# Softmax denominators folded through DRAM instead of on TensorE, and a recurrence started from halves

## The chip, the cores and the metric

The kernel runs on one core of one Trainium2 chip. Its engines have names here: PE (TensorE, the matrix engine; PEld is its weight loads), DVE (VectorE), ACT (ScalarE), POOL (GpSimd) and SP (SyncE, which here only issues DMA transfers). SBUF is the on-chip memory of 128 partitions, PSUM the accumulator that PE writes, DRAM the memory off the core. Everything is float32. The metric is the device time of one execution in microseconds, the median of several.

## What is computed

The input x has 4 batches of 128 channels and 64 x 64 = 4096 positions. Three stages follow one another.

```
# layer 0, per batch, xf = x[b] as (128 channels, 4096 positions)
q, k, v = wq @ xf, wk @ xf, wv @ xf              # 64 rows each
att = softmax(k.T @ q, axis=keys)                # 4096 x 4096
x = x + wo @ (att @ v.T).T
# layer 1, per batch, t = x as (4096 tokens, 128)
h = layernorm(t)
t = t + softmax(causal(h Wq (h Wk).T / sqrt(128))) @ (h Wv)
# last stage, a recurrence over the 4096 tokens of each batch
wx = batchnorm(layernorm(t) @ W.T)               # statistics over all batches and tokens
y[n] = sigmoid(wx[n] + y[n-1] @ V.T),  y[-1] = 0
out = t + y
```

Of each softmax the kernel divides only at the end: it forms the sum of exp(score) x value over the keys, the sum of exp(score) over the keys (the denominator of a query), and multiplies the first by the reciprocal of the second.

## The kernel before

The main program is fast_path. A second one, general_path, is in the program as well and runs only when a flag is set at the end, if a denominator leaves its range or the recurrence has not converged.

**Work items.** For each batch there are 8 blocks of 512 queries in layer 0 and then 8 in layer 1. A block is cut into items of two tiles of 128 keys: 16 items in each block of layer 0, and 2, 4, ... 16 in the causal blocks of layer 1. An item is handled in three steps: scores (L753: PE makes s_ps, ACT takes exp into p), sums (L794: DVE adds p into dsum, L804, or copies it for a block's first item, L802) and values (L814: PE adds p times the values into acc). One slot of the loop at L896 holds scores of item s, values of item s-2 and sums of item s. There are four buffers for p and two of PSUM for s_ps, one for acc, and two ("misc") that all other PE products share.

**The end of a block.** When the last item has its values (L839), ACT copies acc (half at L843 in layer 0, agg at L846 in layer 1), DVE adds the halves (agg, L844) and brings the two halves of dsum together in den (L848): 128 partitions by 512 queries, where a partition holds the sum over the keys that lie on it. What is missing is the sum over the 128 partitions, with the result on the partition of its query. DVE transposes den in squares of 32 x 32 (folded, L556) and adds 32 neighbours (part, L558): part has, on partition 32k + r, for each of the 4 x 4 groups of 32 queries, the sum over the k-th quarter of the keys. In project the matrix fold adds the four quarters on PE (den_ps, L567), and as every partition then holds the sums of its row of all four groups, DVE multiplies by a mask (quarter, L569) and adds (L570) to keep its own group's. The reciprocal follows (recs, L571), the output product o_ps on PE (L574), and the scaled addition into xs (L579). Then comes the layer norm (normed, L588 to L595; POOL takes the power at L455), a transposition into squares (sqT, L609) and an exchange through DRAM that makes the transposed tokens xhT: by_r in layer 0 (L642, L647: four writes, four reads), by_c in layer 1 (L702, L706: four writes, one read). In layer 1 the last step is third (L708): wx_ps on PE, its statistics on DVE (L713), and ACT's copy into xs (L722).

**The order.** These steps are chains of generators: `yield n, step` means that the step comes n slots later; one step runs at the end of a slot, the earliest due first, and if none is due, a task of the side list (the next batch's keys and values). In layer 0 the folding comes one slot after the block's end, the rest (project and what follows) at the end of the next block. In layer 1 the chain is

```
yield 1, first       # folded, project, store to x2, normed
yield 3, second      # squares, exchange
yield 1 if final else 4, third
```

with final the last block of the last batch. From the program so written the framework makes one list of instructions for each engine, with a scheduler of its own that may move an instruction up or down its engine's list where the data allow. Every engine works its list in order, and an instruction that has to wait holds up those behind it. All transfers of the main loop are issued by SP.

**The recurrence** (L972 to L995) is cut into 256 chunks of 16 tokens for each batch, all taken side by side. A chunk's starting state comes from WARM = 12 warm-up steps over the tokens ahead of it. The first has no previous state and is only a sigmoid (L982); every other step is a product on PE (L985), an addition on DVE (L987) and a sigmoid on ACT (L990) for each of the four batches. With the 16 steps proper that makes 28 rounds. At the end the state that a chunk reaches is compared with the one that the next chunk was started from (L1014 to L1025); in_range (L612) counts the reciprocals that lie between two bounds into good. Both set the flag.

Of the kernel before, what the change touches and what calls it, by code (L numbers as in the profile page):

```python
# [349 lines left out]
def fast_path(  # L350
# [27 lines left out]
    TPB = BLK // P  # L378
    SHIFT = 32.0
    LOW, HIGH = 1e-25, 1e25  # L380
    WARM, TOL, STEPS = 12, 1e-6, 16
    NCH = N // STEPS
    CPB = BLK // STEPS
    S = nc.vector.STREAM_SQUARE_SIZE
# [45 lines left out]
    for q in range(1, Q):  # L430
        nc.vector.tensor_copy(fold[:, ts(q, S)], fold[:, :S])

    quarter = const.tile([P, TPB, Q], F32, name="quarter")
    for j in range(TPB):
        nc.vector.tensor_reduce(quarter[:, j], ident.rearrange("p (q r) -> p q r", r=S), AX.X, ALU.add)
# [8 lines left out]
    good = const.tile([P, 1], F32, name="good")  # L444
# [5 lines left out]
    nc.gpsimd.memset(ends[:, 0:1], float((B * NB - 1) * BLK))  # L450
    spare = const.tile([P, 1], F32, name="spare")

    def rsqrt(y, var, z):
# [7 lines left out]
    with tc.tile_pool(name="batch", bufs=1) as batch, tc.tile_pool(name="rows", bufs=2) as rowp, tc.tile_pool(  # L461
# [7 lines left out]
        def misc(name):  # L469
            return ps_m.tile([P, BLK], F32, tag="m", name=name)  # L470
# [2 lines left out]
        wp = misc("warm_ps")  # L473
        for _ in range(12):
            nc.tensor.matmul(wp[:, :P], lhsT=ident, rhs=ident, start=True, stop=True)

        def form():
            gp = misc("g_ps")
# [71 lines left out]
            nc.scalar.copy(r, ps)  # L550
            bs[b].next.append(r)

        def folded(den):

            sq = wk.tile([P, TPB * Q, S], F32, tag="sq", name="sq")
            nc.vector.transpose(out=sq.rearrange("p a b -> p (a b)"), in_=den)  # L556
            part = stat.tile([P, TPB * Q], F32, tag="part", name="part")
            nc.vector.tensor_reduce(part, sq, AX.X, ALU.add)  # L558
            return part

        def project(layer, b, g, agg, part):

            dp = misc("den_ps")
            rec = recs[:, layer, b, ts(g, TPB)]


            nc.tensor.matmul(dp[:, : TPB * Q], lhsT=fold, rhs=part, start=True, stop=True)  # L567
            own = stat.tile([P, TPB, Q], F32, tag="own", name="own")
            nc.vector.tensor_tensor(own, dp[:, : TPB * Q].rearrange("p (j q) -> p j q", q=Q), quarter, ALU.mult)  # L569
            nc.vector.tensor_reduce(rec, own, AX.X, ALU.add)  # L570
            nc.vector.reciprocal(rec, rec)  # L571
            op = misc("o_ps")
            for j in range(TPB):
                nc.tensor.matmul(  # L574
                    op[:, ts(j, P)], lhsT=agg[:, ts(j, P)], rhs=wv1 if layer else wo2, start=True, stop=True
                )
# [35 lines left out]
        def in_range():  # L612

            r = recs.rearrange("p l b t -> p (l b t)")
            r2 = wk.tile([P, BLK], F32, tag="den", name="r2")[:, : 2 * B * NT]
# [3 lines left out]
            nc.vector.tensor_reduce(good, r, AX.X, ALU.add)  # L619

        def ahead():

# [5 lines left out]
        def finish0(b, g):  # L628

            agg, den = bs[b].agg, bs[b].den  # L630

            def norm():
                if g == 0:
                    bs[b].xh = batch.tile([P, NT, P], F32, tag="xh", name="xh")
                    bs[b].xhT = batch.tile([P, N], F32, tag="xhT", name="xhT")
                normed(b, g, bs[b].xh[:, ts(g, TPB)])

            def by_channels():
                sq = squares(bs[b].xh[:, ts(g, TPB)])
                by_r = dram2.tile([S, Q, TPB, Q, S], F32, tag="by_r", name="by_r")  # L640
                for q in range(Q):
                    nc.sync.dma_start(  # L642
                        out=by_r[:, :, :, q].rearrange("r c j t -> r (c j) t"),
                        in_=sq[ts(q, S)].rearrange("r c j t -> r (c j) t"),
                    )
                for c in range(Q):
                    nc.sync.dma_start(  # L647
                        out=bs[b].xhT[ts(c, S), ts(g, BLK)], in_=by_r[:, c].rearrange("r j q t -> r (j q t)")
                    )

            def rest():
                yield 1, norm
                yield 2, by_channels

            def first():
                part = folded(den)

                def second(s):
                    project(0, b, g, agg, part)
                    push(s, rest())  # L660

                fill.append(second)

            yield 1, first

        def finish1(b, g):
# [10 lines left out]
            def first():  # L677
                if final:

                    nc.scalar.activation(spare, agg[:, 0:1], AF.Sigmoid)  # L680
                project(1, b, g, agg, folded(den))
                if final:
                    warm(9, agg[:, : BLK // 2])
                nc.sync.dma_start(
                    out=x2[b, ts(g, BLK)].rearrange("(j p) c -> p j c", p=P),
                    in_=xs[:, b, ts(g, BLK)].rearrange("p (j c) -> p j c", c=P),
                )
                mem["xh"] = wk.tile([P, TPB, P], F32, tag="xh2", name="xh2")
                normed(b, g, mem["xh"])
# [18 lines left out]
            def third():  # L708
                wp = misc("wx_ps")
                nc.tensor.matmul(wp, lhsT=wf, rhs=mem["xhT"], start=True, stop=True)  # L710
                if b == B - 1 and g == NB - 1:
                    in_range()
                nc.vector.bn_stats(ends[:, 3:] if final else stats[:, b * NB + g], wp)  # L713
                if b == B - 1 and g == NB - 2:
                    ahead()

                to = xs[:, b, ts(g, BLK)]
                if final:
                    nc.scalar.copy(to.rearrange("p (s c) -> p s c", c=CPB), wp.rearrange("p (c s) -> p s c", s=STEPS))
                    warm(6, to[:, : BLK // 2])  # L720
                else:
                    nc.scalar.copy(  # L722
                        to.rearrange("p (s j q u) -> p s j q u", q=Q, j=TPB, s=STEPS),
                        wp.rearrange("p (q j u s) -> p s j q u", q=Q, j=TPB, s=STEPS),
                    )

            yield 1, first
            yield 3, second
            yield 1 if final else 4, third


        class Item:
# [163 lines left out]
        for s in range(len(items) + SKEW + 16):  # L896
# [20 lines left out]
            if due:  # L917
                w = min(due, key=lambda w: w[0])
                waiting.remove(w)
                w[1]()  # L920
                push(s, w[2])
            elif side:
                side.pop(0)()
                if not side and items[s].b == 0 and items[s].layer == 0:
                    tokens()
                    load_rest()
        assert not waiting and not side and not fill


# [4 lines left out]
    with tc.tile_pool(name="xr", bufs=1) as xrp, tc.tile_pool(name="y", bufs=2) as yp, tc.tile_pool(  # L934
# [17 lines left out]
        shift = xrp.tile([P, 1], F32, name="shift")  # L952
        nc.vector.tensor_tensor(shift, mv[:, 0:1], scale, ALU.mult)
        nc.vector.tensor_tensor(shift, beta, shift, ALU.subtract)

        by_step = xs.rearrange("p b (g s c) -> p b s g c", s=STEPS, c=CPB)
        start = xrp.tile([P, B, NCH + 1], F32, name="start")
# [14 lines left out]
        def step(b, s):  # L972
# [6 lines left out]
            else:  # L979
                y = states(b, s)  # L980
            if prev[b] is None:
                nc.scalar.activation(grid(y), wx, AF.Sigmoid, scale=scale, bias=shift)  # L982
            else:
                ps = ps_y.tile([P, NCH], F32, tag=f"y{b}", name="y_ps")
                nc.tensor.matmul(ps if s < 1 else pair(ps), lhsT=vf, rhs=prev[b], start=True, stop=True)  # L985
                z = yp.tile([P, NCH], F32, tag=f"z{b}", name="z")
                nc.vector.scalar_tensor_tensor(  # L987
                    grid(z), in0=wx, scalar=scale, in1=grid(ps), op0=ALU.mult, op1=ALU.add
                )
                nc.scalar.activation(y, z if s < 0 else pair(z), AF.Sigmoid, bias=shift)  # L990
# [24 lines left out]
        for b in range(B):  # L1015
# [5 lines left out]
        count = xrp.tile([P, B + 1], F32, name="count")  # L1021
# [68 lines left out]
```

## Time and profile before

| | |
|---|---|
| median of three runs | 2115.99 us (2115.71 to 2116.8) |
| the profiled execution | 2116.78 us, its span in the trace 2115.1 us |
| PE busy | 2081.9 us (98%) |
| DVE busy | 1501.6 us (71%) |
| ACT busy | 1009.5 us (48%) |
| POOL busy | 112.2 us (5%) |
| fold product on PE (L567), 64 times | 128 matmul passes, mean 240 ns |
| product with the mask on DVE (L569) | 64 times, mean 164 ns |
| reduction (L570), reciprocal (L571) | 64 times each, mean 166 and 177 ns |
| dsum additions of 128 x 1024 (L804) | 676 times, mean 1221 ns |
| recurrence step on DVE (L987) | 108 times, mean 480 ns |

The span is the time from the first to the last record; the few microseconds around it belong to the execution too. A line of the profile with an arrow, such as "[0.66 <-ACT p L778]", means that the engine stood idle for 0.66 us and that the event which ended this was ACT writing p. A matmul of float32 is two passes, so counts on PE are twice the program's, and since matmuls are pipelined a pass's own duration overlaps the next; what a product costs PE is seen from one start to the next.

### The profile page before, as it was taken

The numbers are of one execution on the slowest core, as the hardware profiler recorded it, in microseconds if no ns is written. First come the engines' busy times: TensorE is split into PE (matmuls) and PEld (weight loads), VectorE is DVE, ScalarE is ACT, GpSimd is POOL, SyncE is SP. The second block draws the span as 40 slices with busy tenths as digits, with TensorE's granted clock in tenths as the row PEclk, the third lists the DMA queues.
The fourth block names the chain that finished last, engine by engine and source line by source line (L and its number), as shares of the span: only waits on it lengthen the run. The fifth ranks groups of instructions, "written<-read, shape, count | busy, mean of one in ns | idle before, by whom it ended". The sixth has DMA issues, their size and how long they took to land. (4 is left out here: it accounts for less than half of the span.)

```text
span 2115.1 us, 30710 instructions
## 1 busy us (share of the span) xinstructions
PE 2081.9 (98%) x11880; PEld 918.3 (43%) x11880; DVE 1501.6 (71%) x2906; ACT 1009.5 (48%) x1099; POOL 112.2 (5%) x220
## 2 busy tenths in 40 slices
PE   9999999999999999999999999999999999999998
PEld 3333354444333344444333335444433334544456
DVE  4898875555788986545689988554478998754578
ACT  5666633333666643333466653333356664333355
POOL 1000010000000001000000001000000000100000
PEclk9999999999999999999999999999999999999999
DMA  3100022000100012100010002210000001110043
GB/s 111 51 21 12 21 70 60 26 15 15 56 21 15 18 36 70 51 24 15 16 51 15 18 21 62 63 30 15 15 16 15 17 21 26 50 31 15 15 164 161
DMA packets 139897, 81.79 MB, mean 39 GB/s; under 512 B 75248, under 2 KB 123888, under 8 KB 138720
## 3 DMA queue, kind: packets, MB, share of 16 engines
q1 hardware_dynamic: 138736, 79.20, 13.1%
q8 instruction: 95, 1.56, 0.3%
q14 instruction: 58, 0.48, 0.1%
q0 software_dynamic: 288, 0.39, 0.1%
q10 hardware_dynamic: 720, 0.16, 0.0%
HBM read 42.24 MB, written 33.29 MB: 36 GB/s over the span
## 5 line engine op out<-in xcount | busy, mean ns | idle before, releaser
L804 DVE TENSOR_TENSOR dsum<-dsum,p 128x1024 f32<-128x1024 f32 x676 | 825.1, 1221 | 409.9 <-ACT p L780 305.7
L778 ACT ACTIVATE p<-s_ps,nshift 128x1024 f32<-128x1024 f32 x512 | 571.3, 1116 | 350.4 <-PE s_ps L764 292.4
L764 PE MATMUL s_ps<-kr 64*64 64x512 f32 x2048 | 570.4, 594 | 5.0 <-ACT p L778 5.0
L824 PE MATMUL acc<-p,v 64*64 64x512 f32 x4096 | 572.9, 592 | 1.7 <-ACT half L843 1.7
L780 ACT ACTIVATE p<-s_ps 128x1024 f32<-128x1024 f32 (+2 forms) x288 | 274.6, 953 | 555.3 <-PE s_ps L773 526.3
L764 PE MATMUL s_ps<-swap,kr 64*64 64x512 f32 x2048 | 530.2, 594 | 1.0 <-DMA swap<-kr 0.9
L773 PE MATMUL s_ps<-rows,xhT 128*128 128x512 f32 (+3 forms) x1152 | 503.7, 559 | 0.0
L832 PE MATMUL acc<-p,xh 128*128 128x512 f32 (+3 forms) x1152 | 501.9, 558 | 0.2
L832 PEld LDWEIGHTS acc<-p,xh 128*128 128x128 f32 x1152 | 215.8, 190 | 243.1 <-issue 230.4
L773 PEld LDWEIGHTS s_ps<-rows,xhT 128*128 128x128 f32 x1152 | 213.2, 190 | 240.2 <-issue 202.9
L824 PEld LDWEIGHTS acc<-p,v 64*64 64x64 f32 x4096 | 169.4, 133 | 281.9 <-issue 274.0
L764 PEld LDWEIGHTS s_ps<-kr 64*64 64x64 f32 x2048 | 152.3, 133 | 143.6 <-issue 122.4
L764 PEld LDWEIGHTS s_ps<-swap,kr 64*64 64x64 f32 x2048 | 138.6, 133 | 139.3 <-issue 125.3
L455 POOL TENSOR_TENSOR ln_rstd<-ln_var,mhalf 128x4 f32<-128x4 f32 x64 | 66.2, 1035 | 1076.4 <-DVE ln_var L591 1076.4
L812 DVE TENSOR_TENSOR dsum<-dsum,p 128x256 f32<-128x256 f32 (+1 forms) x120 | 55.9, 501 | 75.5 <-POOL p L784 75.5
L579 DVE SCALAR_TENSOR_TENSOR xs<-o_ps,recs,xs 128x128 f32<-128x128 f32 x256 | 71.9, 343 | 7.4 <-PE o_ps L574 3.7
L595 DVE TENSOR_SCALAR xh<-xs,ln_mv,ln_rstd 128x128 f32<-128x128 f32 x256 | 71.4, 342 | 2.3
L784 POOL TENSOR_SCALAR_AFFINE_SELECT p<-p 128x128 f32<-128x128 f32 x128 | 35.2, 299 | 652.2 <-ACT p L780 642.5
L588 DVE BATCH_NORM_STATS2 ln_st<-xs 128x6 f32<-128x128 f32 x256 | 63.4, 269 | 0.0
L722 ACT COPY xs<-wx_ps 128x512 f32<-128x512 f32 x31 | 18.2, 586 | 80.6 <-DVE stats L713 80.6
L802 DVE COPY dsum<-p 128x1024 f32<-128x1024 f32 x60 | 41.1, 686 | 20.2 <-ACT p L780 15.9
L987 DVE SCALAR_TENSOR_TENSOR z<-xs,scale,y_ps 128x256 f32<-128x256 f32 x108 | 48.3, 480 | 3.3 <-PE y_ps L985 1.9
(132 smaller groups left out, 1054.7 us busy)
## 6 DMA issues: line engine op xcount, KB each, us to landing
xs<-in_xT SPq DMA_DIRECT2D x32, 256.0 KB, 3.0
by_r<-sqT SPq DMA_DIRECT2D x128, 64.0 KB, 2.2
xhT<-by_r SPq DMA_DIRECT2D x128, 64.0 KB, 2.0
x<-xs SPq DMA_DIRECT2D x32, 256.0 KB, 2.2
xr<-x SPq DMA_DIRECT2D x8, 1024.0 KB, 12.5
out_x<-xr SPq DMA_DIRECT2D x16, 512.0 KB, 4.4
by_c<-sqT SPq DMA_DIRECT2D x124, 64.0 KB, 1.8
xhT<-by_c SPq DMA_DIRECT2D x31, 256.0 KB, 2.6
```

What stands on the lines that cost most here:

```text
L455: nc.gpsimd.tensor_tensor(y, var, mhalf[:, : y.shape[-1]], ALU.pow)
L579: nc.vector.scalar_tensor_tensor(t, in0=op[:, ts(j, P)], scalar=rec[:, j : j + 1], in1=t, op0=ALU.mult, op1=ALU.add)
L588: nc.vector.bn_stats(st[:, j], xs[:, b, ds(g * BLK + j * P, P)])
L595: nc.vector.tensor_scalar(dst[:, j], xs[:, b, ds(g * BLK + j * P, P)], mv[:, j, 0:1], y[:, j : j + 1], ALU.subtract, ALU.mult)
L764: nc.tensor.matmul(ps[c * M : c * M + M, off : off + n], lhsT=bs[it.b].kr[part, h, ds(t % (NT // 2) * P + c * M, M)], rhs=rows[h], start=True,
L773: nc.tensor.matmul(ps[:, off : off + n], lhsT=lhsT, rhs=rhs, start=True, stop=True)
L778: nc.scalar.activation(it.p[:, :off], ps[:, :off], AF.Exp, bias=nshift)
L780: nc.scalar.activation(it.p[:, :off], ps[:, :off], AF.Exp, scale=float(P) ** -0.5)
L804: nc.vector.tensor_tensor(flat, flat, it.p, ALU.add)
L812: nc.vector.tensor_tensor(den[:, h, q0:], den[:, h, q0:], it.p[:, o : o + n], ALU.add)
L824: nc.tensor.matmul(bt.acc[h * M : h * M + M, r], lhsT=bt.v[part, t], rhs=it.p[part, o : o + n], start=it.first, stop=it.last,)
L832: nc.tensor.matmul(bt.acc[:, 0, q0:], lhsT=bt.xh[:, t], rhs=it.p[:, o : o + n], start=it.first and h == 0, stop=it.last and h == 1,)
```

## The change

Four things are changed in fast_path.

1. In layer 0's blocks, and in layer 1's from the third on (all but the last of the last batch), the four quarters in part are no longer added on PE. part is written to a DRAM tile by_token in four transfers, one from each quarter of the partitions, so that it lies there by token, and read back in one as own: 128 partitions, each with the four quarters of its own four queries. In all that is 32 + 24 - 1 = 55 blocks, each with four writes of 2 KB in pieces of 16 bytes, and one read of 8 KB. The multiplication by the mask is not needed there; the addition of the four (now over quarters) and the reciprocal remain. The nine other blocks keep the product and the mask, with the two dimensions in another order.
2. In layer 1 the chain is given new distances: folding one slot after the block's end, then, where the quarters go through DRAM, first two slots after that; third of the first two blocks comes 6 slots after second instead of 4.
3. The recurrence starts from a state of 0.5 everywhere: V's product with a column of halves is formed once near the start (form_half), added to the bias of the first sigmoid (shift_half), and WARM is 11.
4. The test of the reciprocals' range is done in two parts: all but the last block's four columns after the last block but one, these four at the end.

```diff
-    WARM, TOL, STEPS = 12, 1e-6, 16
+    WARM, TOL, STEPS = 11, 1e-6, 16
...
+        def form_half():
+            hp = misc("h_ps")
+            nc.tensor.matmul(hp[:, 0:1], lhsT=vf, rhs=point5, start=True, stop=True)
+            nc.vector.tensor_copy(v_half, hp[:, 0:1])
...
-        def folded(den):
+        def folded(den, by_pe):
...
-            nc.vector.tensor_reduce(part, sq, AX.X, ALU.add)
-            return part
+            nc.vector.tensor_reduce(part, sq.rearrange("p j q s -> p q j s"), AX.X, ALU.add)
+            own = stat.tile([P, Q, TPB], F32, tag="own", name="own")
+            if by_pe:
+                dp = misc("den_ps")[:, : TPB * Q]
+                nc.tensor.matmul(dp, lhsT=fold, rhs=part.rearrange("p q j -> p (q j)"), start=True, stop=True)
+                nc.vector.tensor_tensor(own, dp.rearrange("p (q j) -> p q j", q=Q), quarter, ALU.mult)
+            else:
+                by_token = dram2.tile([Q, S, Q, TPB], F32, tag="by_token", name="by_token")
+                for k in range(Q):
+                    nc.sync.dma_start(out=by_token[:, :, k].rearrange("q r j -> r q j"), in_=part[ts(k, S)])
+                nc.sync.dma_start(out=own, in_=by_token.rearrange("q r k j -> (q r) k j"))
+            return own
...
-        def project(layer, b, g, agg, part):
-            dp = misc("den_ps")
+        def project(layer, b, g, agg, own):
             rec = recs[:, layer, b, ts(g, TPB)]
-            nc.tensor.matmul(dp[:, : TPB * Q], lhsT=fold, rhs=part, start=True, stop=True)
-            own = stat.tile([P, TPB, Q], F32, tag="own", name="own")
-            nc.vector.tensor_tensor(own, dp[:, : TPB * Q].rearrange("p (j q) -> p j q", q=Q), quarter, ALU.mult)
-            nc.vector.tensor_reduce(rec, own, AX.X, ALU.add)
+            nc.vector.tensor_reduce(rec, own.rearrange("p q j -> p j q"), AX.X, ALU.add)
             nc.vector.reciprocal(rec, rec)
...
             def first():
-                part = folded(den)
+                own = folded(den, False)
                 def second(s):
-                    project(0, b, g, agg, part)
+                    project(0, b, g, agg, own)
...
-                project(1, b, g, agg, folded(den))
+                project(1, b, g, agg, mem["own"])
...
                 if b == B - 1 and g == NB - 1:
-                    in_range()
+                    in_range(True)
...
                 if b == B - 1 and g == NB - 2:
                     ahead()
+                    in_range(False)
...
-            yield 1, first
+            by_pe = final or g < 2
+            def sums():
+                mem["own"] = folded(den, by_pe)
+            if by_pe:
+                yield 1, lambda: (sums(), first())
+            else:
+                yield 1, sums
+                yield 2, first
             yield 3, second
-            yield 1 if final else 4, third
+            yield 1 if final else 6 if g < 2 else 4, third
...
+        shift_half = xrp.tile([P, 1], F32, name="shift_half")
+        nc.vector.tensor_tensor(shift_half, shift, v_half, ALU.add)
...
-                nc.scalar.activation(grid(y), wx, AF.Sigmoid, scale=scale, bias=shift)
+                nc.scalar.activation(grid(y), wx, AF.Sigmoid, scale=scale, bias=shift_half)
```

More of the change, by code (lines that the diff above doesn't have):

```diff
@@ L431, in fast_path @@
         nc.vector.tensor_copy(fold[:, ts(q, S)], fold[:, :S])
-    quarter = const.tile([P, TPB, Q], F32, name="quarter")
+    quarter = const.tile([P, Q, TPB], F32, name="quarter")
     for j in range(TPB):
-        nc.vector.tensor_reduce(quarter[:, j], ident.rearrange("p (q r) -> p q r", r=S), AX.X, ALU.add)
+        nc.vector.tensor_reduce(quarter[:, :, j], ident.rearrange("p (q r) -> p q r", r=S), AX.X, ALU.add)
     wf = const.tile([P, P], F32, name="wf")
@@ L443, in fast_path @@
     wv1 = load(nc.gpsimd, "wv1", [P, P], (whole, a_wv))
-    good = const.tile([P, 1], F32, name="good")
+    good = const.tile([P, 2], F32, name="good")
     g1 = const.tile([P, P], F32, name="g1")
@@ L450, in fast_path @@
     nc.gpsimd.memset(ends[:, 0:1], float((B * NB - 1) * BLK))
+    point5 = const.tile([P, 1], F32, name="point5")
+    nc.gpsimd.memset(point5, 0.5)
+    v_half = const.tile([P, 1], F32, name="v_half")
     spare = const.tile([P, 1], F32, name="spare")
@@ L551, in rows1 @@
             bs[b].next.append(r)
-        def folded(den):
[L555 to L558, printed above, removed]
-            return part
-        def project(layer, b, g, agg, part):
-            dp = misc("den_ps")
+        def folded(den, by_pe):
+            sq = wk.tile([P, TPB, Q, S], F32, tag="sq", name="sq")
+            nc.vector.transpose(out=sq.rearrange("p j q s -> p (j q s)"), in_=den)
+            part = stat.tile([P, Q, TPB], F32, tag="part", name="part")
+            nc.vector.tensor_reduce(part, sq.rearrange("p j q s -> p q j s"), AX.X, ALU.add)
[11 more added lines that the diff above has]
+        def project(layer, b, g, agg, own):
             rec = recs[:, layer, b, ts(g, TPB)]
-            nc.tensor.matmul(dp[:, : TPB * Q], lhsT=fold, rhs=part, start=True, stop=True)
-            own = stat.tile([P, TPB, Q], F32, tag="own", name="own")
-            nc.vector.tensor_tensor(own, dp[:, : TPB * Q].rearrange("p (j q) -> p j q", q=Q), quarter, ALU.mult)
-            nc.vector.tensor_reduce(rec, own, AX.X, ALU.add)
+            nc.vector.tensor_reduce(rec, own.rearrange("p q j -> p j q"), AX.X, ALU.add)
             nc.vector.reciprocal(rec, rec)
@@ L610, in squares, with in_range @@
             return sq
-        def in_range():
+        def in_range(last):
             r = recs.rearrange("p l b t -> p (l b t)")
-            r2 = wk.tile([P, BLK], F32, tag="den", name="r2")[:, : 2 * B * NT]
+            r = r[:, -TPB:] if last else r[:, :-TPB]
+            r2 = wk.tile([P, BLK], F32, tag="den", name="r2")[:, : r.shape[-1]]
             nc.vector.tensor_scalar(r2, r, LOW, None, ALU.is_ge)
@@ L618, in in_range @@
             nc.vector.tensor_tensor(r, r, r2, ALU.mult)
-            nc.vector.tensor_reduce(good, r, AX.X, ALU.add)
+            nc.vector.tensor_reduce(good[:, 1:2] if last else good[:, 0:1], r, AX.X, ALU.add)
         def ahead():
@@ L926, in fast_path @@
                     load_rest()
+                    form_half()
         assert not waiting and not side and not fill
@@ L1020, in fast_path @@
             nc.scalar.activation(sq, ps, AF.Square, accum_out=gap[:, b : b + 1])
-        count = xrp.tile([P, B + 1], F32, name="count")
+        count = xrp.tile([P, B + 2], F32, name="count")
         nc.vector.tensor_scalar(count[:, :B], gap, TOL * TOL, None, ALU.is_le)
```

## The prediction, made before the changed kernel was run

> **What bounds the kernel now.** I read the page's busy shares first, then busy time by stage, then in each stage who waits for whom.
>
> ```profile
> span 2115.1 us, 30710 instructions
> ...
> PE 2081.9 (98%) x11880; PEld 918.3 (43%) x11880; DVE 1501.6 (71%) x2906; ACT 1009.5 (48%) x1099; POOL 112.2 (5%) x220
> ```
>
> PE at 98% says that a PE instruction taken out shortens the kernel. The stages say where that holds: inner blocks of layer 0, long blocks of layer 1, the recurrence.
>
> ```profile
> 139.70:198.60 58.90, 58.30 (x534) 21.51 (x533) 52.82 (x91) 37.49 (x35) 2.02 (x2) 1.00 0.09 19
> 350.00:500.00 150.00, 150.00 (x404) 70.63 (x403) 77.68 (x162) 48.29 (x55) 7.27 (x16) 1.00 0.11 30
> 2038.00:2086.00 48.00, 48.00 (x217) 33.76 (x217) 46.11 (x104) 47.43 (x105) 0.00 (x0) 1.00 0.36 151
> ```
>
> Columns are PE, weight loads, DVE, ACT, POOL, granted clock (1.00: no throttle here), DMA. Layer 1 (second row) is PE's alone: DVE is half idle. The first row is two blocks of layer 0, 58.9 us: PE misses 0.6 us and DVE looks 90% busy, but DVE's waits in that stretch are only these:
>
> ```profile
> DVE ln_z L456 <- POOL ln_rstd L455: 2.2, 2, 1.1
> DVE dsum L804 <- ACT p L778: 0.5, 1, 0.5
> ```
>
> The remaining 3.4 us are gaps of about 0.1 us between its own instructions. So DVE runs through without a pause, and PE follows it: 16 items of 1.715 us and 1.31 us for the denominators' product and o_ps make 28.75 us on PE, but the copies of half, one per block, start 29.47 us apart (169.15, 198.61). In the trace of one block end:
>
> ```profile
> 199.27 0.69 DVE L558 TENSOR_REDUCE part<-sq 128x16 f32<-128x512 f32 x1
> ...
> 200.66 1.23 DVE L804 TENSOR_TENSOR dsum<-dsum,p 128x1024 f32<-128x1024 f32 x1
> 201.81 0.17 DVE L569 TENSOR_TENSOR own<-den_ps,quarter 128x16 f32<-128x16 f32 x1
> 202.01 0.17 DVE L570 TENSOR_REDUCE recs<-own 128x4 f32<-128x16 f32 x1
> 202.21 0.18 DVE L571 RECIPROCAL recs<-recs 128x4 f32<-128x4 f32 x1
> 202.31 0.66 DVE L844 TENSOR_TENSOR agg<-half 128x512 f32<-128x512 f32 x1
> ...
> 204.91 1.19 DVE L804 TENSOR_TENSOR dsum<-dsum,p 128x1024 f32<-128x1024 f32 x1
> ```
>
> Between 199 and 210 DVE sums only three items while PE makes six; ACT then lacks one of the four p buffers (2.60 us of waiting for dsum at 211.38) and PE stops:
>
> ```profile
> 212.54 0.65 PE L764 MATMUL s_ps<-kr 64*64 64x512 f32 x2 [0.66 <-ACT p L778]
> ```
>
> Whatever lengthens DVE's run between the block's end and sqT lengthens the block; a PE saving there is lost.
>
> **The change part by part.** Sums are against the profiled execution, 2116.78 us (span 2115.1 and 1.7 around it), 0.8 above the median of the runs.
>
> *One warm-up round less.* L987 runs 108 times from 2038.5 to 2087.7: 49.2/107 x 4 = 1.84 us a round; among warm-up rounds ACT's starts lie 1.81 apart. PE, DVE and ACT are all full there, so it counts whole: -1.8. What it adds: shift_half on DVE before the first sigmoid, +0.2 (L954 took 0.16 and a gap of 0.03); v_half's product of one column, about a den product, +0.2 once. The range test on 4 columns instead of 256 after the last block: L617 and L618 held up ln_var by about 0.5, small forms cost about 0.3, -0.2; the other 252 columns go into layer 1, where DVE is half idle: 0. Could the start from halves fail the convergence test and call the slow path? Worked out from the reference's inputs in double precision, the largest squared gap is 1.7e-14 with 11 steps from halves, 7.9e-15 with 12 from zero, the bound 1e-12: no. Together -1.6.
>
> *The PE product, 55 of 64 removed.* Its price is from its start to the next matmul's start, not the modelled 240 ns:
>
> ```profile
> 198.32 0.40 PE L567 MATMUL den_ps<-part,fold 128*128 128x16 f32 x2
> 198.56 1.14 PE L574 MATMUL o_ps<-wo,agg 128*128 128x128 f32 x8
> ...
> 427.08 0.29 PE L567 MATMUL den_ps<-part,fold 128*128 128x16 f32 x2
> 427.22 1.14 PE L574 MATMUL o_ps<-wv,agg 128*128 128x128 f32 x8
> ```
>
> 0.24 in layer 0, 0.14 in layer 1. Where PE binds: blocks 2 to 6 of layer 1, 20 x 0.14; block 7 of three batches, 3 x 0.24; layer 0's block 7, whose product falls into layer 1, 4 x 0.33 (at 262.3). That is -4.8. The other 24, in layer 0, are under DVE.
>
> *DVE in layer 0's blocks 1 to 6.* In the changed kernel's instruction order, the product with quarter is gone, and recs<-own, now waiting for a DMA, stands before the dsum of 204.91, not a block later: the framework moved it up. Behind it queue that sum and all sums after it; ACT waits for them, PE for ACT. Without the wait DVE would get there 4.45 us after part's end (199.96): 204.91 less the 0.50 that own, recs and the reciprocal took. The two that stay take about 0.25 in their new places, so a block changes by X - 0.25, X being how long own is late. When does it land? The nearest row is the exchange of layer 1, four writes and a read that waits for them, with 128 packets a write as here:
>
> ```profile
> 435.04 1.76 SPq L702 DMA_DIRECT2D by_c<-sqT  x4
> 438.20 0.34 SPq L706 DMA_DIRECT2D xhT<-by_c  x1
> ```
>
> SP issues 0.04 after DVE is done; the read goes out 3.16 later. By the trace's packets, a write's first packet runs 1.0 after issue, its last ends at 1.4, and SP goes on 0.41 after that; the read's first packet is 1.0 after issue and PE resumed 0.42 after its last. With 2 KB a write for 64 KB, and 8 KB read for 256 KB, packets of 0.4 shrink to 0.1 to 0.2. So own lands at 0.04 + 2.95 + 1.65 = 4.65, X = 0.2. Ends: packets costing nothing, 4.45, X = 0 (at best -0.25 a block); by_c's own 3.16 and the 2.0 that xhT<-by_r takes, 5.2, X = 0.75. I take 0.2, nearest by packets: 4 batches x 5 intervals x -0.05 = -1.0.
>
> The Trainium skill speaks against it: its page "DMA: Bandwidth & Descriptors" (Anatomy of one DMA) gives every DMA a fixed cost of about 2.0 us, most of it the write's receipt, and (Specifications) has pieces under 512 B read, modified and written. The rows agree only in part: by_r's 128 B writes land in 2.1 us, by_c's 512 B in 1.8. By the page, as an estimate, own would land at 0.04 + 1.34 + 2 x 2.0 = 5.4, X = 0.95, and the whole sum would be +7.5.
>
> *The interval from block 6 to block 7 (33.05 us, four times).* There o_ps waited until own had read den_ps:
>
> ```profile
> 231.49 1.16 PE L574 MATMUL o_ps<-wo,agg 128*128 128x128 f32 x8 [1.08 <-DVE own L569]
> ```
>
> That wait and 0.22 for the product go, 1.30. But here recs<-own stands ahead of the scaling (L579), so DVE waits some 2.2 us; following p's buffers as above, ACT's item 23 starts 2.2 late against a PE that is 1.3 ahead, and as 1.16 of such lateness is absorbed (at 211 a delay of 2.0 cost PE 0.84), PE loses 1.04: -0.26 each, -1.0, with bounds -1.3 and +0.4 each.
>
> *Batch boundaries, three.* PE waited 1.9 us for xhT<-by_c at 541.97. In the new chain block 7 of layer 1 is scaled two items later and its wx product too; without o_ps at 526.8 PE's items come 1.3 earlier, and the scaling, from 528.75, moves to about 531.9, xhT's landing from 541.97 to 544.1, PE's arrival from 540.1 to 543.3. Wait 0.8. Between 0 and -1.9 each I take -0.7: -2.1.
>
> *At nothing.* SP issues five more transfers, 2.1 us, 55 times; it is past its loads by then and x<-xs, by_c and by_r queue behind a wait of 1.4 us only; if that cover went, the boundary would lose its 0.7. In layer 1, recs<-own can stop DVE up to 2 us; DVE idles 2.2 us an item there and PE is three buffers away.
>
> Sum: -1.6 - 4.8 - 1.0 - 1.0 - 2.1 = **-10.5**, 2106.3 in the profiled execution, **2105.5** against the median. As a function: -15.3 + 24 X.
>
> **The rivals.** *(1) own lands like by_c, X about 0.65:* sum near 0, no change (within 0.2%, 4.2 us, about what a measurement tells from none). For it: the order of transfers is by_c's; against: a thirtieth of the bytes. *(2) Slower: DVE waits for own.* From X = 0.81 the gain is gone and over. Were 16-byte pieces to cost as by_r's 512 packets do (1.94 to issue, 2.32 to the read's issue, 2.0 to land), own came at 6.3, X = 1.85: +29, 2145. Against: by_token has a quarter of by_r's packets. *(3) Layer 0 is PE's after all:* then 24 products and all four 1.08 waits count too, -18 with the boundaries' -2.1: 2098. The missing DVE idle speaks against it. *(4) The convergence flag sets and the slow path runs as well:* thousands of us; the gaps above exclude it but for an error.
>
> **How the numbers follow.** Mine 0.48 (its own range 2099 to 2112), rival 3 0.10, rival 1 0.21, rival 2 0.20, rival 4 0.01. Faster 0.58, same 0.21, slower 0.21. Low: X = 0 with the boundary waits gone, 2097; high: X = 0.9, 2123.
>
> **What would show it.** Right: recs<-own idle before it near 0.2 us in layer 0, interval of half near 29.4, o_ps without a wait for own, 104 z's. Wrong: recs<-own waiting 0.8 us or more for the DMA, and ACT p's waits for dsum above 51 us; or layer 1 no longer free of PE gaps.

## The result, and the profile after

The changed kernel took 2111.87 us (median of 2114.27, 2111.20, 2109.72 and 2112.54) against 2115.85 for the kernel before beside it: 4.0 us less, ratio 0.9983, 95% interval 0.9966 to 1.0. Timed again in the fifth experiment, with more runs, it took 2110.28 us against 2116.43, 6.2 us less, ratio 0.9971 (0.9959 to 0.9983). The forecast was 10.5 us less. The first interval just reaches no change, the second does not. The sign was right and the time lies in the range, but only four to six tenths of the forecast gain came.

The changed kernel's page begins:

```profile
span 2112.6 us, 30728 instructions
...
PE 2068.2 (98%) x11764; PEld 902.4 (43%) x11764; DVE 1489.1 (70%) x2853; ACT 1007.1 (48%) x1095; POOL 117.9 (6%) x221
```

PE has 13.7 us less work (2081.9 before), but the span is only 2.5 us shorter (2115.1 before): PE stands still for longer than it did. Where, shows the same table by stage as before (columns: PE, weight loads, DVE, ACT, POOL, granted clock, DMA):

```profile
140.05:199.39 59.34, 57.89 (x530) 21.09 (x530) 53.26 (x89) 37.50 (x35) 2.02 (x2) 1.00 0.10 20
350.00:500.00 150.00, 150.00 (x400) 70.34 (x399) 77.18 (x156) 48.50 (x57) 7.79 (x16) 1.00 0.11 31
```

The two blocks of layer 0 that took 58.9 us, 58.30 of them busy on PE, now take 59.34 with 57.89 busy; layer 1 is PE's without a gap as before. DVE's waits in that stretch, and over the whole kernel DVE's wait for own and PE's longest kind of wait:

```profile
DVE ln_z L459 <- POOL ln_rstd L458: 2.2, 2, 1.1
DVE recs L586 <- DMA own<-by_token: 0.6, 2, 0.4
...
DVE recs L586 <- DMA own<-by_token: 40.9, 30, 3.7
...
PE s_ps L791 <- ACT p L805: 21.0, 23, 2.7
```

The columns are the total, the number and the longest. The second wait is new: 30 of the 55 transfers kept DVE waiting. PE's wait for p was 5.0 us before, in 12 places. DVE's waits come through ACT to PE, in the way that the prediction traced for its item at 211 us; ACT's wait for dsum, which it named as a sign of being wrong above 51 us, is now 67.8.

Stage by stage, from the traces, in us. Layer 0 is counted from half copy to half copy. What PE lost by running at half clock (3.41 us at half clock lose 1.71; of that more below) is taken out of the stretches and has a row of its own. It is counted there as if PE had been busy all through, which it was before, and after for 14.5 of the 17.1 us. A last stretch at half clock, at the very end of both executions, is not counted, because PE has no work left in it.

| stretch | before | after | difference |
|---|---|---|---|
| layer 0, blocks 0 to 6, four batches | 699.97 | 705.12 | +5.15 |
| interval from block 6 to 7, four | 132.19 | 130.25 | -1.94 |
| from block 7's half copy to the next batch's first (layer 1), three | 887.03 | 880.52 | -6.51 |
| the rest (start, last layer 1, recurrence, end) | 392.47 | 388.14 | -4.3 |
| half clock | 3.4 | 8.5 | +5.1 |

Everything but the first and the last row came as forecast or better.

One block's end shows the good case. The read of own went out at 677.44 (2.95 after part's end at 674.49), and own had landed when DVE came to it:

```profile
678.88 0.16 DVE L605 BATCH_NORM_AGGREGATE ln_mv<-ln_st 128x2 f32<-128x6 f32 x1
679.08 0.18 DVE L586 TENSOR_REDUCE recs<-own 128x4 f32<-128x16 f32 x1
```

From part's end to recs<-own that is 4.59 us; the forecast had 4.65. The next block, with the same instructions:

```profile
703.75 1.75 SPq L579 DMA_DIRECT2D by_token<-part  x4
706.63 0.34 SPq L580 DMA_DIRECT2D own<-by_token  x1
```

```profile
708.11 0.17 DVE L605 BATCH_NORM_AGGREGATE ln_mv<-ln_st 128x2 f32<-128x6 f32 x1
709.37 0.18 DVE L586 TENSOR_REDUCE recs<-own 128x4 f32<-128x16 f32 x1 [1.09 <-DMA own<-by_token]
```

SP issued on time, yet own came 1.09 us late. The DMA view of the two blocks (674.4 to 680.0, then 703.7 to 709.4) shows the difference. Its queue lines are packets, MB and share; its issue lines end with the median time from issue to landing:

```profile
q1 hardware_dynamic: 720, 0.02, 6.5%
...
own<-by_token SPq DMA_DIRECT2D x1, 8.0 KB, 1.6
...
q1 hardware_dynamic: 720, 0.02, 6.5%
q8 instruction: 1, 0.02, 1.2%
...
own<-by_token SPq DMA_DIRECT2D x1, 8.0 KB, 2.7
```

In the late block one more packet was under way: 16 KB on queue 8, the program's own instructions being loaded, which held one of the 16 DMA engines for 1.13 us. Over the whole kernel there are 94 such loads, one for about 250 of PE's 23528 records (matmul and weight load), and 61 of 8 KB on queue 14. The latter are put down to the other engines, because they stay where they are when PE's are moved (experiment 4). In layer 0 PE's come about every 14.3 us, so two fall into each block, and their place in a block drifts slowly. Of the 28 blocks of layer 0 whose denominators are needed within layer 0, 14 had no load of either kind between part's end and own's landing, and recs<-own began after 4.48 to 4.81 us; in the other 14 it began after 4.97 to 7.03. Undisturbed, the wait X in the inner blocks is 0 to 0.25; over all 16 intervals from block 2 to 6 it was 0.63 on average. These intervals lie within 0.5 us of a line: interval = 29.17 us + 0.91 x wait (the one at 640.97, with half clock in it, left out).

### The profile page after: what moved, and what is told of

It is laid out like the page before. It is cut to its first block, busy times and chain, and to the rows that moved or that the text cites. A ratio compares the mean times of both kernels' runs of the same rounds, so it can differ in the third digit from the quotient of the medians.

```text
span 2112.6 us, 30728 instructions
## 1 busy us (share of the span) xinstructions
PE 2068.2 (98%) x11764; PEld 902.4 (43%) x11764; DVE 1489.1 (70%) x2853; ACT 1007.1 (48%) x1095; POOL 117.9 (6%) x221
## 5 line engine op out<-in xcount | busy, mean ns | idle before, releaser
L791 PE MATMUL s_ps<-kr 64*64 64x512 f32 x2048 | 530.6, 595 | 16.7 <-ACT p L805 16.7
L851 PE MATMUL acc<-p,v 64*64 64x512 f32 x4096 | 534.0, 592 | 1.7 <-ACT half L870 1.7
L851 PEld LDWEIGHTS acc<-p,v 64*64 64x64 f32 x4096 | 155.3, 133 | 286.1 <-issue 272.7
L791 PEld LDWEIGHTS s_ps<-kr 64*64 64x64 f32 x2048 | 138.0, 133 | 157.5 <-issue 118.0
L811 POOL TENSOR_SCALAR_AFFINE_SELECT p<-p 128x128 f32<-128x128 f32 x128 | 40.4, 339 | 551.7 <-ACT p L807 546.0
L459 DVE TENSOR_TENSOR ln_z<-ln_rstd 128x4 f32<-128x4 f32 x64 | 10.5, 164 | 67.5 <-POOL ln_rstd L458 67.5
```

Of the source, the lines that this page charges most:

```text
L791: nc.tensor.matmul(ps[c * M : c * M + M, off : off + n], lhsT=bs[it.b].kr[part, h, ds(t % (NT // 2) * P + c * M, M)], rhs=rows[h], start=True,
L851: nc.tensor.matmul(bt.acc[h * M : h * M + M, r], lhsT=bt.v[part, t], rhs=it.p[part, o : o + n], start=it.first, stop=it.last,)
```

## The experiments

My theory after the result: the sure gains came, and layer 0 gave them back, because recs<-own stands early in DVE's list and own is late whenever a code load crosses its transfers. The rival: layer 0 is not at fault, and the gains elsewhere were smaller than forecast.

**1. The recurrence alone.** The kernel before, with

```diff
-    WARM, TOL, STEPS = 12, 1e-6, 16
+    WARM, TOL, STEPS = 11, 1e-6, 16
...
+                    form_half()
...
+        nc.vector.tensor_tensor(shift_half, shift, v_half, ALU.add)
```

> The kernel before with only the third change: the recurrence starts from halves and has one warm-up round less. My theory of the result (the sure gains came as forecast, layer 0 gave them back) expects this part at its forecast price, a round of 1.84 us less 0.4 for its product and its addition: about -1.5 us, 2114.4. The rival, that the gains themselves were smaller than forecast, expects less than half of that, 2115.3 or more.

Measured: 2113.96 us against 2115.89, -1.9, ratio 0.9992 (0.9983 to 1.0001). The size is what the theory expects; the interval just reaches no change, so it is not proof by itself.

**2. Only layer 1 through DRAM.**

```diff
-                own = folded(den, False)
+                part = folded(den, None)
...
-                    project(0, b, g, agg, own)
+                    project(0, b, g, agg, gathered(part, True))
```

gathered is the product with fold and the mask, in its old place.

> The changed kernel, but layer 0's blocks add their quarters on PE in the place where the kernel before does it; layer 1, its chain, the halves and the range test are as changed. Theory: layer 0, whose intervals grew by 4.9 us in sum with the change, goes back, and the gains of layer 1 and of the recurrence stay: 1.6 + 20 x 0.14 + 3 x 0.24 + 2.1 = 7.2 us under the kernel before, 2108.8, so 3 us faster than the changed kernel. Rival (layer 0 is not where the missing gain went, the parts in layer 1 were worth less): between 2111 and 2113, no faster than the changed kernel.

Measured: 2105.59 us, -10.3, ratio 0.9952 (0.9939 to 0.9966): 4.7 to 6.3 us faster than the changed kernel. So layer 0 is where the gain went. It is 3 us better than my sum, and the trace tells why, for the execution that was profiled: the boundary waits of PE fell to 1.4 to 1.5 us from 1.8 to 1.9, and with them went both of the half-clock stretches that the kernel before has in its main loop (1.71 each).

**3. The reciprocal held back.** The transfers stay as they are; only DVE's two instructions are put behind the ninth dsum of the next block.

```diff
             rec = recs[:, layer, b, ts(g, TPB)]
-            nc.vector.tensor_reduce(rec, own.rearrange("p q j -> p j q"), AX.X, ALU.add)
-            nc.vector.reciprocal(rec, rec)
+            with tc.issue_after(late.ins) if late else ExitStack():
+                nc.vector.tensor_reduce(rec, own.rearrange("p q j -> p j q"), AX.X, ALU.add)
+                nc.vector.reciprocal(rec, rec)
```

> The changed kernel with one difference in layer 0: the addition recs<-own and its reciprocal are held back in DVE's list until behind the ninth dsum of the next block, about 15 us after the transfers began, so that own has landed long before. All transfers stay. Theory (DVE's wait for own is what layer 0 lost): no wait before recs in the inner blocks, half copies 29.2 us apart as in the changed kernel's blocks that did not wait (29.63 on average there), 20 x 0.45 = 9 us, and 1 to 2 us in each of the four intervals from block 6 to 7: 2095 to 2099. Rival (the transfers disturb layer 0 by themselves, or it is bound by something else): intervals stay near 29.6, 2110 to 2112.

Measured: 2085.4 us, -30.5, ratio 0.9848 (0.9834 to 0.9861), 25 to 26 us faster than the changed kernel. DVE's waits from the first to the seventh half copy of the third batch are now

```profile
DVE dsum L833 <- ACT p L807: 6.0, 13, 0.5
DVE ln_z L459 <- POOL ln_rstd L458: 5.6, 5, 1.1
```

and nothing for own, where the changed kernel has 6.0 us. That DVE waits 6.0 us for ACT's p (3.3 in the changed kernel) says that it now runs ahead of ACT. The table by stage, for two inner blocks:

```profile
138.45:196.84 58.39, 57.89 (x530) 21.12 (x530) 52.96 (x89) 37.52 (x35) 2.02 (x2) 1.00 0.11 20
```

The transfers, with all their lateness, cost nothing once nobody waits for them in the wrong place: the rival of a disturbance by the transfers themselves is out. The gain is larger than I expected, because the intervals from 6 to 7 fell to 30.58 us each, from 32.56 on average in the changed kernel and 33.05 before; I had expected 1 to 2 less. Blocks 0 to 6 went from 705.12 to 691.0.

**4. The code loads moved.** 32 products of one column ahead of everything, so that each later load of PE's instructions comes 128 instructions earlier against the work:

```diff
+        for _ in range(32):
+            nc.tensor.matmul(wp[:, :1], lhsT=ident, rhs=ones, start=True, stop=True)
```

> The changed kernel with 32 one-column products more on PE ahead of everything (their results are not used), which moves every later load of PE's instructions 128 instructions, in layer 0 some 7.2 us, earlier against the blocks. In the changed kernel own was late in just those blocks where a 16 KB load of PE's code, or an 8 KB one of another engine's, came within 5 us after part's end. Theory (the code loads make own late): the waits of recs<-own leave batch 2's blocks 2 to 5 (0.88 to 1.18 us now, under 0.3 then) and come to batch 0's blocks 2 to 5 (0.64 at most now; 0.8 or more in two of them then). Rival (the lateness is chance or comes from the transfers' own traffic): the waits stay where they are or come anywhere. The total: within 3 us of the changed kernel by either.

Measured: 2115.08 us, 3 to 5 more than the changed kernel, a little beyond what was expected; the products put the first half copy 12.3 us later, 6.8 of it lost at half clock. The waits did what the theory said. Block 3 in batch 0 and in batch 2, the changed kernel first, then this one:

```profile
146.14 0.18 DVE L586 TENSOR_REDUCE recs<-own 128x4 f32<-128x16 f32 x1 [0.18 <-DMA own<-by_token]
...
1152.46 0.18 DVE L586 TENSOR_REDUCE recs<-own 128x4 f32<-128x16 f32 x1 [1.08 <-DMA own<-by_token]
```

```profile
160.03 0.18 DVE L588 TENSOR_REDUCE recs<-own 128x4 f32<-128x16 f32 x1 [0.96 <-DMA own<-by_token]
...
1162.60 0.18 DVE L588 TENSOR_REDUCE recs<-own 128x4 f32<-128x16 f32 x1
```

The DMA view of the same two blocks in this kernel (154.5 to 160.1, then 1158 to 1163): the load is now in the first and gone from the second.

```profile
q8 instruction: 1, 0.02, 1.0%
...
by_token<-part SPq DMA_DIRECT2D x4, 2.0 KB, 2.5
...
by_token<-part SPq DMA_DIRECT2D x4, 2.0 KB, 1.5
```

Blocks 2 to 5 of batch 0 wait 1.24, 0.96, 1.23 and 0.99 us (0.64, 0.18, 0.40 and 0.25 in the changed kernel); blocks 2 to 5 of batch 2 wait 0.02 at most (1.18, 1.08, 0.88 and 0.91). Nothing but the phase of the code had been moved. The 8 KB loads stayed where they were (in blocks 2 and 4 of batch 0 they begin 4.0 and 2.1 us after part's end in both kernels). That the code loads make own late is thereby shown. Here, too, the intervals from block 2 to 6 lie within 0.4 us of a line, 29.12 + 1.04 x wait.

**5. The changed kernel again.**

> The changed kernel itself, timed again beside the others: four runs of it lay 4.0 us under the kernel before, while its trace, stage by stage and with the time in which PE's clock was halved taken out, lies 6.8 under. Theory: layer 0 has taken back most of the gain, so 4 to 7 us under, 2109 to 2112. Were the change worth nothing, it would lie within 2 us of 2116.

Measured: 2110.28 us, -6.2, as given above; its trace has DVE waiting for own 31 times, 40.5 us in all, and the waits of layer 0 come back in the same blocks, within 0.5 us. The 6.8 that was expected from the stages counts as lost also the half clock at the end, where PE has no work; by the table above it is 7.6.

**6. Only layer 0 through DRAM.** The kernel before, with layer 0's folding and project as changed, and nothing else.

```diff
-                part = folded(den)
+                part = by_dram(den)
...
+            if layer == 0:
+                return project0(b, g, agg, part, rec)
```

> The kernel before, with layer 0's quarters through DRAM as in the change and nothing else (layer 1 with its product and its chain, twelve warm-up rounds from zero). Theory: the first seven blocks of a batch lose 5.2 us in sum as in the changed kernel's trace, the intervals from block 6 to 7 win 1.95, and 1.3 for the four products that fell into layer 1: +2.0, 2118 (2116 to 2120), slower than before though a product is gone. Rival (layer 0's part is a gain and something else in the change ate it): 2108 to 2114.

Measured: 2117.17 us, +0.7, ratio 0.9999 (0.999 to 1.0008). It is no gain, though 32 products have left PE. Layer 1's part, together with the recurrence's (experiment 2), is worth 10 us, layer 0's nothing. My +2 was a little high: 10 of the 28 blocks met a load here, 14 in the changed kernel, and the first seven blocks sum to 702.5 instead of 705.1. Nor do the parts add up exactly (-10.3 and +0.7 against -4 to -6 for the whole): which blocks wait, and where PE loses its clock, differs from program to program.

**7. One hop more.**

```diff
+                near = folded(den, False)
+                own = stat.tile([P, Q, TPB], F32, tag="own2", name="own2")
+                nc.sync.dma_start(out=own, in_=near)
```

> The changed kernel, with one more transfer in layer 0 between the read-back and recs<-own (SBUF to SBUF, the same 8 KB), so that own lands some 1.7 us later (from the read's issue to DVE's release it takes 1.65 in an undisturbed block). Nothing else. Theory (a microsecond of waiting costs a block 0.9 to 1.0 us: over blocks 2 to 5 the intervals of the changed kernel lie on 29.15 + 0.91 to 1.04 times the wait): 20 x 1.6 for the inner blocks and 4 x 1.0 to 1.7 for the intervals from 6 to 7, +36 to +39 over the changed kernel, 2147 to 2152. Rival (the wait is for the most part absorbed by the buffers of p behind it, as I put it for the interval from 6 to 7): under +15.

Measured: 2155.96 us, +45.7 over the changed kernel, ratio to before 1.0181 (1.0166 to 1.0195).

```profile
DVE recs L586 <- DMA own<-own: 78.5, 29, 4.1
...
PE s_ps L793 <- ACT p L807: 54.2, 26, 3.2
```

The waits went from 40.9 to 88.8 us (with 10.3 more for by_token, in layer 1). The sum is a little above my 36 to 39, but made up differently. With the half clock taken out, the 20 inner intervals grew by 35.9 us for 42.8 us more waiting, 0.84 for one (I had put 32 for 32); the four intervals from 6 to 7 did not grow by 4 to 7 but shrank by 2.6, and the wait for own in them did not grow either (9.0 us in sum, 9.8 in the changed kernel); and PE lost 13.7 us more at half clock, which I had not counted. So the rival is out for the inner blocks; on the interval from 6 to 7 this run says nothing. One of this kernel's waits of PE, and the table for three stretches: the wait itself, the next 3.4 us and the 3.4 us after those (the clock is third from the end):

```profile
706.82 0.66 PE L793 MATMUL s_ps<-kr 64*64 64x512 f32 x2 [2.81 <-ACT p L807]
```

```profile
703.90:706.80 2.90, 0.11 (x4) 0.00 (x0) 2.79 (x3) 1.11 (x1) 0.00 (x0) 1.00 0.27 42
707.30:710.70 3.40, 3.40 (x22) 1.05 (x18) 3.19 (x3) 1.91 (x2) 0.00 (x0) 0.50 0.33 71
710.80:714.20 3.40, 3.40 (x40) 1.19 (x36) 3.09 (x4) 2.20 (x2) 0.00 (x0) 1.00 0.12 31
```

In its main loop this trace has 12 such stretches at half clock; the changed kernel's has 2.

**8. The wait for the power moved back as well.** To the third experiment's kernel:

```diff
-                yield 1, norm
-                yield 2, by_channels
+                yield 2, norm
+                yield 1, by_channels
...
+        with tc.issue_after(late.ins) if late else ExitStack():
+            nc.vector.tensor_tensor(z, y, y, ALU.mult)
```

> The kernel with the late reciprocals (recs<-own behind the ninth dsum) and one thing more: DVE's wait of 1.12 us a block for POOL's power (ln_z<-ln_rstd), the last wait left in its list in layer 0, is taken away too, by holding ln_z back behind one more dsum (the step norm one slot later, the exchange in its old slot). Theory: at 29.08 us a block DVE still set the pace there, PE needs 28.75 - 0.24 = 28.5: 20 x 0.4 to 0.55 and a little in the last interval, 2075 to 2078. Rival (PE sets the pace of these blocks once the wait for own is gone): no faster than the late reciprocals alone, 2085.

Measured: 2080.66 us, ratio 0.9829 (0.9816 to 0.9842), 4.7 faster than the third and the best of all. It is less than the forecast of 7 to 10. The two inner blocks show why:

```profile
110.91:168.34 57.43, 57.43 (x530) 21.32 (x530) 52.29 (x89) 37.55 (x35) 3.83 (x2) 1.00 0.11 20
```

PE has no gap left and takes 28.72 us a block, not the 28.5 that I had worked out; layer 0 is now PE's. DVE's wait itself is not gone, as I had expected it to be. It only comes later in the list:

```profile
DVE ln_z L460 <- POOL ln_rstd L458: 1.8, 2, 0.9
```

POOL's power took 1.91 us in these two blocks, 1.01 in the third experiment's, and DVE still waits 0.9 us for it in each (1.1 there). What fell are ACT's waits for DVE's dsum and den: 1.2 us in these two blocks, 2.9 for dsum alone in the third experiment's two. It is the place of the wait that counted, as with own.

**9. On PE, but in the middle of a block.** The second experiment's kernel, with product, mask and reciprocal as a step of its own:

```diff
+            def middle():
+                inverse(recs[:, 0, b, ts(g, TPB)], gathered(mem[0], True))
...
             yield 1, first
+            yield 1 if g == NB - 1 else 7, middle
```

> The kernel of the second experiment (layer 0's quarters added on PE, everything else as changed), but the product, the mask and the reciprocal of a block are a step of their own in the middle of the next block instead of standing at its end, ahead of o_ps. No transfers in layer 0. It asks what of the 25 us that the late reciprocals won is owed to the way through DRAM. Theory (placement won them, DRAM saves only PE's product and DVE's mask): layer 0 at 28.94 to 29.3 us a block, o_ps no longer waiting for own, the interval from 6 to 7 near 30.8; 0.2 to 0.25 more than the late reciprocals in 24 intervals and 0.33 in four: 2091 to 2093. Rival (the transfers are what took the load off layer 0): near the second experiment, 2102 to 2106.

Measured: 2099.15 us, ratio 0.9923 (0.9909 to 0.9938). It lies between the two theories: of the 20.2 us from the second experiment to the third, placement alone wins 6.4, and the way through DRAM, well placed, 13.8. I had put the latter at 6 to 8. In the middle of a block the product costs PE 0.48 us and not 0.24: inner blocks take 29.20 with PE full (busy 117.02 of 117.02 us over four of them), 0.48 above the 28.72 of the eighth experiment.

## Why the prediction was wrong

*The step that failed is the size of X*, how long own is late in layer 0's inner blocks. The prediction took 0.2, from by_c's packets and SP's issues, "20 x (X - 0.25)" = -1.0; the stretch it speaks of cost +5.15. The mechanism, the place and the price of a microsecond were right: recs<-own waits there, ACT lacks p, PE stops, and an interval grows by 0.84 to 1.04 us for each of waiting. Without a wait it is 29.12 to 29.17 us against 29.47 before, 0.30 to 0.35 less, so the 0.25 was nearly right too. Even the undisturbed landing was: 4.65 forecast, 4.48 to 4.81 measured. What was missing is a second distribution beside it. In about half of the blocks a load of instructions crosses the five small transfers and adds 0.3 to 2.4 us. The rows from which I worked out X were one exchange in an undisturbed moment; the trace of before held the loads as well, and the prediction has no term for them. The page of before has them in this line (packets, MB, share):

```profile
q8 instruction: 95, 1.56, 0.3%
```

The forecast function, -15.3 + 24 X, gives -0.2 at the measured X of 0.63. The profiled execution's span gained 2.5 instead: the inner blocks lost 5.2 where the function then has 7.6, the intervals from 6 to 7 won 1.9 where it has a loss of 0.7, the other stages won 10.8 where it has 8.5, and the half clock, which it does not have, took 5.1.

The Trainium skill's estimate in the prediction (X = 0.95 from a fixed cost of 2.0 us for every DMA) was nearer to the mean, for another reason: undisturbed, own took 1.55 to 1.8 us from its issue to DVE's start, all told less than that fixed cost. The section of "DMA: Bandwidth & Descriptors" that the prediction names (Anatomy of one DMA) is headed as that of transfers issued by GpSimd, and these are issued by SP; for every transfer the figure stands in "SBUF — State Buffer" (The DMA setup-cost knee). The 2.1 us set against it for by_r is the median of its writes and reads together; its writes alone take 2.2. The skill's page "Runtime: NRT & Kernel Launch" (Instruction fetch mechanics) says that instructions come in blocks of 16 KiB, 256 of them, through a DMA queue of the sequencer's own, and that the cost is mostly hidden. The blocks agree with the 16 KB rows; the cost is hidden from the engine whose code it is (PE was busy 150.00 of 150 us between 350 and 500 us, with three such loads in them), and was not from the transfers of the kernel beside it.

The other steps:

- *One round less, -1.6:* measured alone, -1.9. 104 z's as forecast, no slow path.
- *The product where PE binds, -4.8, and the batch boundaries, -2.1:* both lie in the stretches of layer 1. An undisturbed one went from 295.70 to 293.17, -2.5, where my terms make 2.0 each. PE's wait for xhT<-by_c went from 1.9 to 1.5 in two of three, not to 0.8; in the third it rose to 3.2. So the boundary gave less than its term; that the products gave the rest, more than theirs, was not measured apart.
- *The interval from 6 to 7, -1.0:* -1.94. o_ps no longer waits (229.53, right behind the copy), DVE waits 2.0 to 3.0 for own, forecast 2.2. That a wait of 2.2 would leave a small gain was right; without the wait each gains 2.5 (experiment 3).
- *Nothing in layer 1:* right, PE has no gap between 350 and 500 us.
- *PE's own time for a block of layer 0, 28.75:* 0.2 too low. Where DVE does not set the pace, the interval from block 1 to 2, it was 28.94 before and is 28.72 without the product. The working left out about 0.17 that PE loses on going over to den_ps and o_ps and back (0.97 us from the last values to the product where 0.86 is the rule, 0.48 instead of 0.43 behind the first scores). It changes no term of the sum.
- *The clock:* not in the prediction at all. PE's new waits of 2.7 us (for ACT's p, at 654) and 3.2 us (for xhT<-by_c, at 1549) were followed by half clock, of 3.41 and 6.83 us; before, two waits of 1.8 and 1.9 us for xhT were, with 3.41 each. A third stretch, 6.83 us from 2029.2, stands at the start of the recurrence; experiment 1, which has no transfer for the denominators, has it too. In sum that is 5.1 us more than before in the profiled execution, the rest of the miss: 2.5 us of span gained where the stages, without it, won 7.6.
- *Rival 1* (X about 0.65, sum near 0) is what happened by its number, though not by its cause, packets as slow as by_c's.

## What to carry to other kernels

A latency read from one transfer is the best case: look in the trace also for what else uses the DMA engines, the loads of instructions among them, and give a wait on a small transfer slack (here 0.3 to 2.4 us were missing in half of the blocks). When an in-order engine has to pick up something that comes by DMA, look in its final list for where the pick-up stands, not in the program: here a list order that cost nothing to change was worth 25 us, and without it half of the change was worth nothing. And a product removed from PE is worth what follows from its place: 0.14, 0.24 or 0.48 us for the same 16 columns.

## What the runs showed of the hardware that was not expected

- Loads of instructions delay small transfers. A 16 KB load takes one DMA engine 0.9 to 1.8 us, mostly under 1.4; five transfers of 16- and 64-byte pieces that cross it land 0.3 to 2.4 us later, and moving the code by 128 instructions moves the lateness to other blocks.
- Waits of PE well below 3.4 us can cost clock. In the 11 traces, between 60 and 2020 us, every stretch at half clock (3.41 us, sometimes 6.83) began within 4.2 us of the beginning of a PE gap of 1.8 us or more. Of 90 shorter gaps (0.9 to 1.78 us) none was followed by one, of 14 gaps up to 2.1 us six were, of 20 longer ones 17. Behind 2020 us three traces have a stretch of 6.83 us after gaps of at most 1.4 us, at the start of the recurrence, so the length of the gap alone does not decide. The Trainium skill's page "TensorE: Matmul & The Clock Gate" (Part 1) puts it down to an idle window of about 3.4 us; the length of the stretches agrees with that, the gaps that suffice were shorter. What else decides, these runs do not show.
- The same product with fold costs PE twice as much between two items (0.48 us) as at a block's end beside o_ps (0.24). In experiment 9's trace, at 128.09 us, 0.32 lie between its start and the next scores; 0.11 more come ahead of it (0.97 from the values to it, 0.86 to scores) and 0.06 behind (0.49 instead of 0.43). The last two, 0.17, o_ps has at the block's end in any case (0.97 and 0.48). They stand where PE goes over from 64 x 64 to 128 x 128 products and back; that this is the reason was not tried.
